# Summing the last experts' results in a graph and mixture-of-experts kernel: GpSimd's additions go to VectorE and TensorE, and three one-hot matrices are made earlier

## The chip, the cores and the metric

The kernel runs on one core of a Trainium2 chip. The metric is the device time of one execution in microseconds; a change is judged by the median of several executions.

## What is computed

The reference takes 384 nodes of 512 features and 6144 edges and applies eight layers, each added to its input. Seven of them (four graph layers, three feed-forward ones) lie before the change. The last one is a mixture of 64 experts, of which each node uses 8:

```python
w, idx = _gate(x2, gate_w, gate_b)          # 8 of 64 experts and their weights, for each node
h = silu(einsum('ecd,edm->ecm', xb, w1)) * einsum('ecd,edm->ecm', xb, w3)
yb = einsum('ecm,emd->ecd', h, w2)
y = yb.at[flat_e, pos].get(...) * w.reshape(-1)[:, None]
return y.reshape(T, K, DIM).sum(1)          # each node: the sum of its 8 weighted results
```

The change is in that last sum over a node's results and the addition to `x`. All data is fp32 at this point.

## The kernel before

The 384 nodes are three tiles of 128 rows (`NT = 3`); `x[:, t, :]` is the running result, 128 x 512 for each tile `t`. The experts are sorted by how many nodes chose them. Expert 0 of that order is computed densely; the other 63 form 38 blocks of at most 128 rows, each of one expert (128 rows) or of two (64 rows each). The loop over `BLOCKS` near line 1616 takes one block per turn. Block 34 is of one expert, 35 and 36 are of two, and 37, the last, is of one.

In turn i the loop does, in this order: start the loads of later experts (SP's DMA queue), gather the rows of block i+4 (GpSimd, indirect DMA), `hidden(i)` on TensorE (tile `mm`), the SiLU on ScalarE and the product `hide` on VectorE, `turned(i+1)` (TensorE, tile `tp`, copied to `xe` by ScalarE), then `output(i-1)`: TensorE multiplies by the second weight and VectorE scales the rows by the routing weight into `ye`. Then `turned_hidden(i)` turns `hide` on TensorE and VectorE copies it to `hT`.

Up to block 34, `output` ends with a scatter by GpSimd: each row of `ye` goes to its own place in `parts`, a DRAM tensor of 384 x 8 rows. For the last three blocks (`DIRECT = 3`) there is no scatter. Instead `placed` makes a one-hot matrix on VectorE (tile `turn`, 128 x 384: which node each row belongs to), and TensorE multiplies it with `ye` into `sums[t]`, one accumulator in PSUM for each tile.

At the end of turn 35 `gathered_back(t)` brings `parts` back: for each tile two DMAs of 1 MB on SP's queue, each with four of the node's eight rows, into the weight buffers that have come free (so the profile names them `w<-parts`). For tiles 0 and 1 GpSimd then adds the second half to the first (128 x 2048 elements). After the loop VectorE adds the four remaining rows of each tile to `x` (`summed`), while for tile 2 the second half is added on TensorE, by multiplying with the identity into `sums[2]`. Last, VectorE adds `sums[t]` to `x[:, t, :]`, and ScalarE's queue stores it to `out`.

What sets the order: from line 1197 on every engine's instructions are issued in the order in which the program writes them (the class `InTurn`, whose helper is line 88; so most lines of the profile show L88, and operations must be told apart by their tiles). SP's queue likewise takes its DMAs in the order written. An engine that waits holds all that is written behind it on that engine.

Profile names: `mm`, `acc` accumulators; `ye` scaled results; `hT` the turned hidden; `turn` the one-hot; `x<-x,w` the additions of returned rows on VectorE; `acc<-w,ident` those on TensorE; `acc<-ye,turn` the matmuls of `placed`; `w<-w,w` the additions on GpSimd; `x<-x,acc` the last sums.

Of the kernel before, what the change touches and what calls it, by code (L numbers as in the profile page):

```python
# [8 lines left out]
F32 = mybir.dt.float32  # L9
# [4 lines left out]
OP = mybir.AluOpType  # L14
AX = mybir.AxisListType

P = 128
N = 384
# [24 lines left out]
DIRECT = 3  # L43
# [6 lines left out]
BLOCKS, _ones, _left = _ones[:3], _ones[3:], _twos[:]  # L50
# [43 lines left out]
def gnn_ffn_kernel(ctx: ExitStack, tc: tile.TileContext, a, out: bass.AP):  # L94
    nc = tc.nc
    V, S, G, T = nc.vector, nc.scalar, nc.gpsimd, nc.tensor
# [5 lines left out]
    def slot(i=None):  # L102

        if i is None:
            i, turns_of_slots[0] = turns_of_slots[0] % W_BUFS, turns_of_slots[0] + 1
        return wpool.tile([P, 4 * D], F32, name=f"w8_{i}")
# [20 lines left out]
    x = const.tile([P, NT, D], F32, name="x")  # L127
# [79 lines left out]
    def row(name, n=D, pool=None):  # L207

        v = a[name]
        r = (pool or rows).tile([P, n], F32, name="row" if pool is None else "row_" + name)  # L210
        nc.scalar.dma_start(r, bass.AP(tensor=v.tensor, offset=v.offset, ap=[[0, P], [1, n]]))
        return r
# [4 lines left out]
    ident = const.tile([P, P], F32, name="ident")  # L217
# [5 lines left out]
    nodes = const.tile([P, N], F32, name="nodes")  # L223
# [96 lines left out]
    with ExitStack() as s1:  # L320
# [102 lines left out]
        with tc.tile_pool(name="pa", bufs=1, space=bass.MemoryType.PSUM) as pa:  # L423
# [19 lines left out]
            sums, counts = {}, []  # L443
# [39 lines left out]
            for c in range(EC):  # L483
# [34 lines left out]
                for h in range(by_scalar(c)):  # L518
                    j = ep.tile([P, 2 * HD0], F32, name="junk", bufs=2)
                    summed = S.activation(j, g3[:, h, :], AF.Identity, accum_out=w8[:, h:h + 1])  # L520
                marks.append(summed)

                with tc.issue_after(done.ins):
# [16 lines left out]

            plain = T, V, S, G
            T, V, S, G = (InTurn(tc, *e) for e in zip(plain, (counts[-1], done, summed, scattered)))
            wv = stream.take(ahead=False)

# [49 lines left out]
    with ExitStack() as s2:  # L594
# [321 lines left out]
        T, V, S, G = plain  # L916
# [26 lines left out]
    for i in range(3):  # L943
# [3 lines left out]
        if i > 0:  # L947
            w = stream.take()
            pw = [ps.tile([P, D], F32, name="mm") for t in range(NT)]
            for k in range(KC):  # L950
                for t in range(NT):
                    T.matmul(pw[t], lhsT=hT[:, k, t * P:(t + 1) * P], rhs=w[:, k, :], start=k == 0,  # L952
                             stop=k == KC - 1)
# [7 lines left out]
        back = [ps.tile([P, D], F32, name="mm") for t in range(NT)] if i == 2 else None  # L961
        for f in range(KC):
# [8 lines left out]
            j = qp.tile([P, N], F32, name="sq")  # L971
# [67 lines left out]
    with tc.issue_after(shown.ins):  # L1039
        b = row("L2_gnn_b")  # L1040
# [25 lines left out]
    moe = ctx.enter_context(tc.tile_pool(name="moe", bufs=2))  # L1066
# [101 lines left out]
    b = row("L3_gnn_bias")  # L1168
# [28 lines left out]
    T, V, S, G = (InTurn(tc, engine) for engine in plain)  # L1197
# [142 lines left out]
    for b in BLOCKS:  # L1340
        for r in b:
            if r >= STATIC:
                free.sort()
                end, i = free.pop(0)
# [3 lines left out]
    def load(i):  # L1348

        for r, n, end in firsts.pop(i, []):  # L1350
            load_expert(r, n)
            seconds.append((r, n, end))
        while seconds and seconds[0][2] + 2 <= i and (len(seconds) > 2 or not firsts):
            r, n, end = seconds.pop(0)
            load_second(r, n)
# [36 lines left out]
    tables, chosen, sources, numbers = {}, {}, {}, {}  # L1392
# [30 lines left out]
    def numbered(g, p):  # L1423

        blocks = GROUPS[g]
        n = len(blocks)
        num = ex.tile([P, n], F32, name=f"num{g}", bufs=1)
        none = ex.tile([P, n], F32, name=f"none{g}", bufs=1)
        src = ex.tile([P, n], I32, name=f"src{g}", bufs=1)
        node = ex.tile([P, n], F32, name=f"node{g}", bufs=1)  # L1430
        for h, c in enumerate(parts_of(blocks)):
            V.tensor_reduce(num[c], p[c, :, h, 0:2], AX.X, OP.add)
        V.tensor_scalar(none, num, 0.0, FAR, op0=OP.is_equal, op1=OP.mult)
        V.scalar_tensor_tensor(node, num, -1.0, none, op0=OP.add, op1=OP.add)
        V.tensor_copy(src, node)
        numbers[g] = num, none, node
        for i, b in enumerate(blocks):
            sources[b] = src[:, i:i + 1]
# [19 lines left out]
    def gather(i):  # L1458
        G.indirect_dma_start(out=rows_of[i % AHEAD], out_offset=None, in_=xnd,
                             in_offset=bass.IndirectOffsetOnAxis(ap=sources[BLOCKS[i]], axis=0),  # L1460
                             bounds_check=N - 1, oob_is_err=False)

    def turned(i):
        p = pt.tile([P, KC, P], F32, name="tp")
        r = rows_of[i % AHEAD].rearrange("c (p k) -> c k p", k=KC)
        for k in range(KC):
            T.transpose(p[:, k, :], r[:, k, :], ident)
        xe = ex.tile([P, KC, P], F32, name="xe")
        S.copy(xe, p)
        return xe  # L1470
# [4 lines left out]
    def hidden(b, xe):  # L1475
        p = ps.tile([P, 2, 2 * P], F32, name="mm")
        for k in range(KC):
            for c, r in zip(halves(b), b):
                T.matmul(p[c], lhsT=xe[:, k, c], rhs=experts_w[r][0][:, :, k, :], start=k == 0, stop=k == KC - 1)
        hid = ex.tile([P, 2 * P], F32, name="hide")  # L1480
        S.activation(hid, p[:, 0, :], AF.Silu)
        V.tensor_mul(hid, hid, p[:, 1, :])
        return hid
# [25 lines left out]
    def placed(i, ye):  # L1509

        b = BLOCKS[i]
        if not sums:
            sums.extend(ps2.tile([P, D], F32, name="acc") for t in range(NT))
        to = moe.tile([P, N], F32, name="turn", bufs=2)
        V.tensor_scalar(to, nodes, tables[b][2], None, op0=OP.is_equal)
        for t in range(NT):
            T.matmul(sums[t], lhsT=to[:, t * P:(t + 1) * P], rhs=ye, start=b == BLOCKS[-DIRECT],
                     stop=t < 2 and b == BLOCKS[-1])

    view = parts.rearrange("(t p j) d -> t p j d", t=NT, p=P)  # L1520
    back = []

    def gathered_back(t):

        halves_ = []
        for h in range(2):
            i = rooms.pop(0)
            r = (slot(i) if i < W_BUFS else more[0].tile([P, 4 * D], F32, name=f"w8_{i}")).rearrange(
                "p (j d) -> p j d", j=4)
            nc.sync.dma_start(r, view[t, :, 4 * h:4 * h + 4, :])  # L1530
            halves_.append(r)
        if t < 2:
            first, second = halves_
            G.tensor_tensor(first, first, second, op=OP.add)
        back.append(halves_)

    def summed(t):
        for j in range(4):
            V.tensor_add(x[:, t, :], x[:, t, :], back[t][0][:, j, :])


    place = moe.tile([P, NT, E3], F32, name="place", bufs=1)
# [7 lines left out]
    def ranked(turn, dst):  # L1550
        p = ps.tile([P, NT, E3], F32, name="mm")
        for t in range(NT):
            T.matmul(p[:, t, :], lhsT=turn[:, t * P:(t + 1) * P], rhs=perm, start=True, stop=True)
        S.copy(dst, p)
# [56 lines left out]
    sums = []  # L1611
# [4 lines left out]
    for i, b in enumerate(BLOCKS):  # L1616


        load(i)
        if 2 <= i and i + AHEAD < len(BLOCKS):  # L1620
            gather(i + AHEAD)
        hid = hidden(b, xes.pop(i))
        if i + 1 < len(BLOCKS):
            xes[i + 1] = turned(i + 1)
        if i == 0:
            numbered(4, told_slots(4, slice(0, 2)))
            gather(3)
            gather(4)
            ranked(turns[1], weight)
        if i in told_at:  # L1630
            to_use = told_at[i], told_slots(told_at[i])
            chosen.pop(told_at[i])

        if i == 1:
            table(*to_use)
            to_use = None
        if i == EXCEED:
            exceeded()
        sent = output(*waiting) if waiting is not None else None
        waiting = i, turned_hidden(hid)  # L1640
        if sent is not None:
            placed(*sent)
        if to_use is not None:
            table(*to_use)
            to_use = None
        if i == 0:
            tell(place0, pick, slice(0, STATIC))
        if i == 1:
            choose(1)
            tell(place, weight, slice(STATIC, E3))  # L1650
        if i == 2:
            gather(5)

        for j in range(i + 1, min(i + AHEAD + 3, len(BLOCKS))):
            g = group_of[BLOCKS[j]]
            if i >= 3 and g not in known and i + 1 not in told_at:
                known.add(g)
                choose(g)
                told_at[i + 1] = g
        if i + 1 == EXCEED:  # L1660
            V.tensor_scalar(hasb, place, 0.5, None, op0=OP.is_gt)
        if i == len(BLOCKS) - DIRECT:
            free.sort()
            rooms = [n for _, n in free]
            for t in range(NT):
                gathered_back(t)
    summed(0)
    placed(*output(*waiting))
    for j in range(4):
        T.matmul(sums[2], lhsT=ident, rhs=back[2][1][:, j, :], start=False, stop=j == 3)  # L1670
    summed(1)
    summed(2)
    for t in range(NT):
        V.tensor_add(x[:, t, :], x[:, t, :], sums[t])
        nc.scalar.dma_start(out[t * P:(t + 1) * P, :], x[:, t, :])
    T, V, S, G = plain
# [71 lines left out]
```

## Time and profile before

| | us |
|---|---|
| median of 3 runs (lowest to highest) | 853.11 (850.22 to 855.66) |
| profiled execution, its own time | 855.45 |
| span of that execution in the trace | 853.5 |
| TensorE, VectorE, ScalarE, GpSimd busy | 746.5, 462.1, 273.1, 234.5 |
| six returning transfers `w<-parts`, median from issue to landing | 11.6 |
| GpSimd's two additions of 128 x 2048 | 4.50 and 4.88 |
| last sum of VectorE ends | 847.97 |

The span is the time between the first and the last recorded event; the execution's own time has 1.95 us around it. Times in the trace count from the span's start. Each record has an engine, an operation, the tiles it writes and reads, its duration, and the idle time of its engine before it with the event that ended it. A matmul of fp32 data is recorded as two passes, so "x6" of `acc<-ye,turn` is three matmuls. Records that the timeline merges in one row carry the time from the first's start to the last's end. "issue" in the chain of waits is time for which the profile shows no cause. The granted clock of TensorE is 1.00 at full speed.

### The profile page before, as it was taken

The numbers are of one execution on the slowest core, as the hardware profiler recorded it, in microseconds if no ns is written. First come the engines' busy times: TensorE is split into PE (matmuls) and PEld (weight loads), VectorE is DVE, ScalarE is ACT, GpSimd is POOL, SyncE is SP. The second block draws the span as 40 slices with busy tenths as digits, with TensorE's granted clock in tenths as the row PEclk, the third lists the DMA queues.
The fourth block names the chain that finished last, engine by engine and source line by source line (L and its number), as shares of the span: only waits on it lengthen the run. The fifth ranks groups of instructions, "written<-read, shape, count | busy, mean of one in ns | idle before, by whom it ended". The sixth has DMA issues, their size and how long they took to land.

```text
span 853.5 us, 9894 instructions
## 1 busy us (share of the span) xinstructions
PE 746.5 (87%) x2865; PEld 350.2 (41%) x2865; DVE 462.1 (54%) x1199; ACT 273.1 (32%) x1042; POOL 234.5 (27%) x230
## 2 busy tenths in 40 slices
PE   5999888898946769948789999799999999999975
PEld 3444433343434535423355544454444344333432
DVE  4575988887779665376522254745434242421227
ACT  1144766666638723333131111221111111011100
POOL 0046777777600210000100000023333233322122
PEclk9999999899968678985989999889999999999998
DMA  9987877877388011210531463298999999999982
GB/s 336 410 312 243 284 273 258 285 216 238 106 330 311 1 37 53 96 50 12 226 138 49 154 215 108 90 390 320 408 408 403 400 387 396 385 389 391 379 338 104
DMA packets 71197, 211.84 MB, mean 248 GB/s; under 512 B 11615, under 2 KB 16351, under 8 KB 70368
## 3 DMA queue, kind: packets, MB, share of 16 engines
q1 hardware_dynamic: 40592, 135.56, 41.7%
q0 software_dynamic: 19728, 57.97, 19.8%
q10 hardware_dynamic: 10816, 17.61, 5.9%
q8 instruction: 25, 0.41, 0.2%
q14 instruction: 36, 0.29, 0.1%
HBM read 188.46 MB, written 29.83 MB: 256 GB/s over the span
## 4 chain that ended last, share of the span: by engine, by line
PE 56%; DVE 20%; DMA 14%; ACT 6%; issue 3%; DVEq 0%; POOL 0%; SPq 0%; ACTq 0%; POOLq 0%
PE mm L88 14%; DMA w<-in_L_ffn_w_dram 11%; PE acc L88 9%; PE mm L290 8%; PE mm L461 6%; PE mm L1080 4%; PE acc L1093 3%; PE tp L88 3%; PE mm L463 2%; PE mm L952 2%; DVE gp L507 2%; PE acc L965 2%; ACT junk L520 2%; DVE gp L509 2%; DVE mx L88 2%
## 5 line engine op out<-in xcount | busy, mean ns | idle before, releaser
L88 PE MATMUL mm<-w,xe 128*64 128x512 f32 (+1 forms) x504 | 146.1, 598 | 4.9 <-DMA w<-in_L_ffn_w_dram 4.9
L461 PE MATMUL mm<-w,osT 128*128 128x512 bf16 x378 | 92.2, 391 | 9.9 <-ACT osT L386 9.8
L88 POOL DMA_INDIRECT xg<-xnd,src x38 | 39.3, 1034 | 164.9 <-DVE ye L88 140.8
L88 ACT ACTIVATE hide<-mm 128x256 f32<-128x256 f32 x38 | 14.6, 385 | 214.1 <-PE mm L88 214.1
L88 POOL DMA_INDIRECT parts<-ye,dst x35 | 37.9, 1083 | 154.9 <-DVE ye L88 154.9
L88 PEld LDWEIGHTS mm<-w,xe 128*64 128x64 f32 (+1 forms) x504 | 48.2, 148 | 75.0 <-issue 69.1
L88 PE MATMUL acc<-w,hT 128*64 128x512 f32 (+1 forms) x244 | 77.4, 610 | 0.0
L88 DVE TENSOR_TENSOR hide<-hide,mm 128x256 f32<-128x256 f32 x38 | 16.1, 424 | 109.0 <-ACT hide L88 109.0
L290 PE MATMUL mm<-w,xT 128*128 128x512 f32 x144 | 68.6, 633 | 1.8 <-DMA w<-in_L_gnn_Ww_dram 1.2
L520 ACT ACTIVATE junk<-gp 128x128 f32<-128x128 f32 x186 | 54.8, 296 | 39.8 <-issue 22.9
L436 POOL DMA_INDIRECT gq<-qd,dsti x48 | 50.6, 1054 | 59.8 <-DMA qd<-gq 41.8
L461 PEld LDWEIGHTS <-osT 128*128 128x128 bf16 x378 | 36.7, 100 | 65.8 <-issue 17.1
L446 POOL DMA_INDIRECT mat<-w,kidx x48 | 57.0, 1187 | 22.5 <-DMA mat<-w,kidx 4.4
L88 DVE TENSOR_SCALAR ye<-acc,wts 128x512 f32<-128x512 f32 x35 | 26.3, 750 | 59.4 <-PE acc L88 59.4
L520 ACT ACTIVATE junk<-relu 128x128 f32<-128x128 f32 x147 | 43.4, 297 | 18.3 <-DVE relu L516 10.6
L290 PEld LDWEIGHTS mm<-w,xT 128*128 128x128 f32 x144 | 28.8, 204 | 37.7 <-issue 34.4
L516 DVE SCALAR_TENSOR_TENSOR relu<-mm,wa_relu 128x512 f32<-128x512 f32 x42 | 28.1, 684 | 29.3 <-PE mm L463 29.3
L463 PE MATMUL mm<-gq,ident 128*128 128x512 f32 x84 | 43.2, 596 | 0.0
L88 PEld LDWEIGHTS tp<-ident,xg 128*128 128x128 f32 x164 | 23.6, 202 | 28.5 <-issue 24.5
L465 PE MATMUL pc<-od,os 128*128 128x384 bf16 x144 | 29.3, 330 | 6.3 <-DVE od L372 6.3
L520 ACT ACTIVATION_READ_ACCUMULATOR junk<-gp 128x1 f32 x186 | 34.8, 187 | 0.0
L509 DVE SCALAR_TENSOR_TENSOR gp<-gp,wa_relu 128x1024 f32<-128x1024 f32 x27 | 33.1, 1228 | 0.9
(370 smaller groups left out, 1210.0 us busy)
## 6 DMA issues: line engine op xcount, KB each, us to landing
w<-in_L_ffn_w_dram SPq DMA_DIRECT2D x204, 512.0 KB, 12.0
mat<-y ACTq DMA_DIRECT2D x2, 4608.0 KB, 28.4
m<-mat SPq DMA_DIRECT2D x12, 768.0 KB, 7.1
parts<-xg POOLq DMA_DIRECT2D x1, 6144.0 KB, 19.9
w<-parts SPq DMA_DIRECT2D x6, 1024.0 KB, 11.6
w<-in_L_gnn_Ww_dram SPq DMA_DIRECT2D x4, 1024.0 KB, 10.1
w<-in_L_gnn_W_dram ACTq DMA_DIRECT2D x2, 1024.0 KB, 9.0
qd<-gq SPq DMA_DIRECT2D x3, 516.0 KB, 6.7
```

The costliest lines, as they stand in the source:

```text
L88: self.last = getattr(self.engine, name)(*args, **kwargs)
L290: last = T.matmul(p, lhsT=xT[:, k, t * P:(t + 1) * P], rhs=w(k), start=start and k == 0, stop=stop and k == kc - 1)
L436: G.indirect_dma_start(out=gq, out_offset=None, in_=qd, in_offset=bass.IndirectOffsetOnAxis(ap=dsti[:, c:c + 1], axis=0))
L446: return G.indirect_dma_start(out=mats[c % 2], out_offset=bass.IndirectOffsetOnAxis(ap=kidx[:, c:c + 1], axis=0), in_=sums.pop(c), in_offs ...
L461: T.matmul(z[h], lhsT=osT[:, t, :], rhs=split[t][:, i, cs], start=t == 0 and i == 0, stop=False)
L463: T.matmul(z[h], lhsT=ident, rhs=gq[:, cs], start=False, stop=True)
L465: counts.append(T.matmul(pc[t], lhsT=os_[:, t * P:(t + 1) * P], rhs=od, start=c == 0, stop=c == EC - 1))
L509: done = V.scalar_tensor_tensor(g3, g3, 0.0, wide, op0=OP.max, op1=OP.mult)
L516: done = V.scalar_tensor_tensor(g3[:, c8, :], z[h].rearrange("p (h k) -> p h k", h=HH), 0.0, wide[:, c8, :], op0=OP.max, op1=OP.mult)
L520: summed = S.activation(j, g3[:, h, :], AF.Identity, accum_out=w8[:, h:h + 1])
L1080: T.matmul(p, lhsT=gate[:, k, c], rhs=xT[:, k, :], start=k == 0, stop=k == KC - 1)
L1093: T.matmul(p, lhsT=hid[:, m, t * P:(t + 1) * P], rhs=w2[:, m, :], start=m == 0, stop=m == 1)
```

## The change

GpSimd's additions are removed. For tiles 0 and 1 VectorE adds all eight returned rows; for tile 2 TensorE adds five by the identity and VectorE three. Five of the additions of tile 0 are issued at the end of turn 36, ahead of block 37's `hide` on VectorE; the others follow the loop, around the last `output`. The one-hot matrices of blocks 35, 36 and 37 are made at the end of turn 34 by a new function `destined`, with one more buffer (`to`).

```diff
@@ placed
-        to = moe.tile([P, N], F32, name="turn", bufs=2)
-        V.tensor_scalar(to, nodes, tables[b][2], None, op0=OP.is_equal)
+        to = tos[b]
@@ gathered_back
-        if t < 2:
-            first, second = halves_
-            G.tensor_tensor(first, first, second, op=OP.add)
         back.append(halves_)
-    def summed(t):
-        for j in range(4):
-            V.tensor_add(x[:, t, :], x[:, t, :], back[t][0][:, j, :])
+    def added_back(t, js):
+        for j in js:
+            V.tensor_add(x[:, t, :], x[:, t, :], back[t][j // 4][:, j % 4, :])
+    def added_too(t, js):
+        for j in js:
+            T.matmul(sums[t], lhsT=ident, rhs=back[t][j // 4][:, j % 4, :], start=False, stop=j == js[-1])
+    tos = {}
+    def destined(b):
+        tos[b] = moe.tile([P, N], F32, name="to", bufs=1) if len(tos) == 2 else             moe.tile([P, N], F32, name="turn", bufs=2)
+        V.tensor_scalar(tos[b], nodes, tables[b][2], None, op0=OP.is_equal)
@@ the loop over the blocks, at the end of a turn
+        if i == len(BLOCKS) - DIRECT - 1:
+            for b in BLOCKS[-DIRECT:]:
+                destined(b)
         if i == len(BLOCKS) - DIRECT:
             free.sort()
             rooms = [n for _, n in free]
             for t in range(NT):
                 gathered_back(t)
-    summed(0)
+        if i == len(BLOCKS) - 2:
+            added_back(0, range(5))
+    added_back(0, range(5, 8))
+    added_back(1, range(3))
     placed(*output(*waiting))
-    for j in range(4):
-        T.matmul(sums[2], lhsT=ident, rhs=back[2][1][:, j, :], start=False, stop=j == 3)
-    summed(1)
-    summed(2)
-    for t in range(NT):
+    added_too(2, range(3, 8))
+    added_back(1, range(3, 8))
+    for t in range(NT):
+        if t == 2:
+            added_back(2, range(3))
         V.tensor_add(x[:, t, :], x[:, t, :], sums[t])
         nc.scalar.dma_start(out[t * P:(t + 1) * P, :], x[:, t, :])
```

## The prediction

> **What bounds the kernel now.** I read the page's chain first, then the chain of waits of the last 35 us, then the timeline of each engine there, then each transfer's landing, then the windows with the granted clock. The diff touches nothing before about 805 us, and the instruction order of every engine and queue up to there is the same in both kernels, so the first 805 us stay as they are. Up to 813.5 us the chain is the stream of expert weights: TensorE waits last on `w<-in_L_ffn_w_dram`. From there nothing more is loaded from the weights, and the end is set by three engines handing blocks 35, 36 and 37 to one another. The chain there, in columns start, duration, what:
>
> ```profile
> 829.38 0.03 DVE ye L88
> 829.42 0.64 issue
> 830.05 0.41 DVE hT L88
> 830.47 2.21 DVE turn L88
> 832.67 0.61 DVE x L88
> 833.29 0.02 issue
> 833.31 4.89 DVE x L88
> 838.20 0.02 issue
> 838.22 0.70 DVE x L88
> 838.92 0.02 issue
> 838.95 0.04 DVE x L88
> 838.98 0.57 issue
> 839.56 0.74 DVE ye L88
> ```
>
> Two pieces stand out: a one-hot (`turn`) of 2.2 us and one addition of 4.9 us, where their neighbours take 0.41 and 0.70. The timeline of GpSimd and VectorE says why:
>
> ```profile
> 827.96 4.50 POOL L88 TENSOR_TENSOR w<-w,w 128x2048 f32<-128x2048 f32 x1 [14.55 <-DMA w<-parts]
> ...
> 830.38 2.29 DVE L88 TENSOR_SCALAR turn<-nodes,node 128x384 f32<-128x384 f32 x1
> 832.60 7.04 DVE L88 TENSOR_TENSOR x<-x,w 128x512 f32<-128x512 f32 x4
> 832.73 4.54 PE L88 MATMUL acc<-ye,turn 128*128 128x512 f32 x6 [2.96 <-DVE turn L88]
> 832.76 4.88 POOL L88 TENSOR_TENSOR w<-w,w 128x2048 f32<-128x2048 f32 x1 [0.30 <-DMA w<-parts]
> ```
>
> The one-hot ends when GpSimd's first addition ends (832.46), and the 4.9 us addition when its second does (837.64). VectorE stands still under GpSimd, and TensorE behind VectorE: its 2.96 us wait is on `turn`. The windows' row shows that this also cost clock (columns: window, length, busy time of PE, PEld, DVE, ACT, POOL, granted clock, DMA share, GB/s):
>
> ```profile
> 829.80:832.70 2.90, 0.00 (x0) 0.00 (x0) 2.90 (x4) 0.00 (x0) 2.65 (x1) 1.00 1.01 421
> 832.70:837.10 4.40, 4.37 (x6) 1.83 (x7) 4.37 (x2) 0.00 (x0) 4.34 (x1) 0.61 0.65 266
> 838.98:840.68 1.70, 0.01 (x1) 0.00 (x1) 1.70 (x4) 0.00 (x0) 0.00 (x0) 1.00 0.00 0
> ```
>
> After 2.9 us without a matmul, six passes took 4.4 us at a clock of 0.61; after 1.7 us the next six took 2.68 (840.68 to 843.36) at 1.00.
>
> **When the data comes back.** The six 1 MB transfers of `parts` are issued at 818.6, 819.0, 819.5, 820.0, 820.7 and 821.5 and need 5.5, 8.6, 10.6, 12.6, 14.4 and 16.1 us to land: 824.1, 827.6, 830.1, 832.6, 835.1, 837.6. The second, asked for alone:
>
> ```profile
> L1530 SPq DMA_DIRECT2D w<-parts x1: 424/424/424, 819.0 to 819.0; - x1
> ...
> DMA to landing us min/median/max: 8.6/8.6/8.6
> ```
>
> GpSimd, which waited for it, began at 827.96, so a landing is seen 0.1 to 0.4 us after that figure. SP waits for the last scatter to land before it issues the first (its longest wait there is 7.2 us on `parts<-ye,dst`); neither is moved, so these six times hold for the new kernel.
>
> **The change, step by step.**
>
> *The three one-hots go in front, to VectorE after 805.2 us.* They cost 3 x 0.33 (step of one to the next, 820.73 to what follows, is 0.33 to 0.41) = 1.0 to 1.2 us where VectorE is idle for 4.17 us, until `hide` at 809.41. Cost nothing; without that cover it would be 1.2 us. [...]
>
> *What stands free on TensorE.* `placed` of block 35 no longer waits for its one-hot (done 821.15), only for `ye` (820.48): 0.65 us earlier. `hidden` of block 37 then ends at 826.75, not 827.40, and its `hide` could run on VectorE at 827.28.
>
> *The new wait.* VectorE now has five additions of tile 0 in front of that `hide`: four on the first transfer (seen 824.1 to 824.5, done by 827.3), the fifth on the second (827.96, as GpSimd saw it), done at 828.66. Behind it stand `hide`, `ye` of block 36, `hT` of block 37, and TensorE's transposes of `hide`. `hide` ends at 829.06, so the transposes start at 829.16; before they started at 829.27. The 0.65 us are thus given back almost wholly, and the cover is gone: any later landing of that transfer moves everything after it.
>
> *Block 36.* `ye` 829.08, `hT` 829.75 (0.67 after it, as in 829.38 to 830.05), done at 830.08. No one-hot follows, so `placed(36)` starts on TensorE at 829.88 instead of 832.73: 2.85 us gained. With a gap of 0.2 us and not 2.9, it runs at full clock: 3 x 0.86 = 2.57 us, to 832.45; block 37's output follows, and `ye` starts 1.95 us later (1.92 to 1.99 in earlier blocks), at 834.4.
>
> *VectorE meanwhile.* Three additions of tile 0 and three of tile 1 (third transfer, 830.1): 830.08 + 6 x 0.70 = 834.3. It is ready just as the output is, so `ye(37)` starts at 834.4 instead of 839.56: 5.15 us gained, of which 1.9 + 4.2 = 6.1 are the two stalls, less additions that GpSimd no longer makes.
>
> *The end.* `placed(37)` runs on TensorE from 835.2 to 837.77, its one-hot being there. Then five, not four, additions by the identity (10 passes of 0.43, the last 0.59) take to 842.2; the one on the fifth transfer comes first (835.1), those on the sixth from 838.6 (landed 837.6, 0.6 us of slack at the least). VectorE: 835.1 + 5 x 0.70 = 838.6, two sums by 839.8, three additions by 841.9, and the last sum waits for TensorE until 842.56 (0.33 after its end, as before: 846.96 to 847.29). Before it started at 847.29: 4.7 us gained. TensorE's fifth addition costs 0.86 of that.
>
> *The store.* The three output transfers were issued at 846.82, 847.41 and 848.4; the second issue took 0.84 us and held the third 0.4 us, and the third landed in 3.3 us where the first took 2.5. Now the first two leave near 839.3 and 839.9, so the third is alone: 0.4 + 0.7 = 1.1 us more at most.
>
> Sum: 4.7 + 1.1 = 5.8 us. The profiled execution took 855.45 us (span 853.5); it would be 849.65. The median of the runs is 853.11, 2.3 below it; since the end of the kernel repeats in each, I take the same 5.8 off: **847.3 us**, 0.7% faster. VectorE has 19 additions for 12 and still ends earlier.
>
> **Rivals.**
>
> [...]
>
> *VectorE becomes the bound.* Additions beside transfers at 420 GB/s might cost more than the 0.70 of rows taken when DMA stood still. From the fifth on, twelve stand on VectorE's chain before the transfers and their neighbours end (1 + 6 + 5); with 0.65 us of slack (841.9 to 842.56) each 0.1 us more costs up to 1.2. At 0.35 more each the gain is 5.8 - 12 x 0.35 + 0.65 = 2.25: 850.9 us. Against it: `hide` took 0.42 under 420 GB/s, as elsewhere.
>
> *Slower: the second transfer is late.* One mechanism, at the fifth addition: `hide`, `ye`, `hT` and TensorE's transposes are queued behind it, so each us by which it is seen after 827.96 adds one. From 833.8 (15.2 us to landing and not 8.6) the gain is used up. That takes transfers that share the engines in turn and land together near 836: 855.3 us, with 2.2 us lost. Against it: the landings are about 2.5 us apart, one after the other.
>
> *The change doesn't do what it says* would be 853 us: stalls with another cause than GpSimd. The two ends that coincide speak against it.
>
> **How the numbers follow.** The forecast 0.74, the clock 0.10, VectorE as the bound 0.08, no effect 0.04, the late transfer 0.04. Runs of the kernel before lie from 850.2 to 855.7, so a median of a few may be off by 2 us, and landings are seen 0.4 us early or late: the forecast alone reaches from 844.2 to 850.0. To hold 8 in 10 over the cases the range is **844.0 to 851.5 us**, which takes in the clock's case and most of VectorE's. A measurement can tell about 1% from no change, 8.5 us here: faster than 844.6 needs more gain than the path has, or luck in the runs (0.11); slower than 861.6 needs the late transfer at its worst (0.03); the rest, 0.86, is within 1%.
>
> **What would show it.** Right: no GpSimd instruction after 813; 19 `x<-x,w` additions of about 0.70, with DMA in the idle column before them; `hide` of block 37 released by VectorE's fifth addition near 828.7; `placed(36)` near 829.9 with a clock of 1.00; `ye(37)` near 834.4; last sum near 842.6; span near 847.7. Wrong: additions of 1 us or more beside transfers, a clock under 1 after 835, a second landing after 829, or a later first issue of the six transfers on SP.

## The result, and the profile after

| | before | after |
|---|---|---|
| median of 22 runs each, us | 852.1 | 845.47 |
| ratio after to before (95% interval) | | 0.9937 (0.9918 to 0.9956) |
| span of the profiled execution, us | 853.5 | 847.5 |
| first matmul after the last weights | 813.52 | 813.58 |
| last sum ends | 847.97 | 842.86 |
| from the end of the last sum to the end of the span | 5.53 | 4.64 |

The ratio is a gain of 5.4 us (3.7 to 7.0). The two traces run within 0.06 us of each other up to the last weights, so all of the 6.0 us by which the spans differ lies behind 813.5: 5.17 in the hand-over of the last blocks and 0.89 in the store. The chain of waits of the changed kernel (start, duration, what) is now TensorE almost without a break:

```profile
828.79 0.76 DVE ye L88
829.55 0.04 issue
829.59 2.84 PE acc L88 x6
832.43 1.73 PE mm L88 x4
834.16 0.03 issue
834.19 0.76 DVE ye L88
834.95 0.04 issue
834.99 7.15 PE acc L88 x16
842.14 0.02 issue
842.17 0.69 DVE x L88
```

VectorE's pieces of 2.2 and 4.9 us are gone, and what remains of it here is `ye`, twice, and the last sum. The timeline of VectorE shows the additions in their new places (start, duration, operation, idle before it and who ended that):

```profile
824.15 2.87 DVE L88 TENSOR_TENSOR x<-x,w 128x512 f32<-128x512 f32 x4 [3.28 <-DMA w<-parts]
827.30 0.69 DVE L88 TENSOR_TENSOR x<-x,w 128x512 f32<-128x512 f32 x1 [0.28 <-DMA w<-parts]
827.91 0.41 DVE L88 TENSOR_TENSOR hide<-hide,mm 128x256 f32<-128x256 f32 x1
828.79 0.75 DVE L88 TENSOR_SCALAR ye<-mm,wts 128x512 f32<-128x512 f32 x1 [0.46 <-PE mm L88]
829.45 0.41 DVE L88 COPY hT<-tp 128x256 f32<-128x256 f32 x1
829.78 4.19 DVE L88 TENSOR_TENSOR x<-x,w 128x512 f32<-128x512 f32 x6
834.19 0.75 DVE L88 TENSOR_SCALAR ye<-mm,wts 128x512 f32<-128x512 f32 x1 [0.22 <-PE mm L88]
```

Block 37's `hide` follows the fifth addition at once and ends at 828.32. TensorE's transposes of it start at 828.67, right behind the matmuls before them and without a wait:

```profile
828.67 0.50 PE L88 MATMUL tp<-ident,hide 128*128 128x128 f32 x2
```

So the wait that the change added is covered, by about a third of a microsecond. VectorE's six additions end 0.22 us before the output for `ye(37)` is there. The returned rows' additions on VectorE from 804 us on (busy time and mean in ns), and windows of TensorE (granted clock third from the end, then the DMA's share and its GB/s):

```profile
L88 DVE TENSOR_TENSOR x<-x,w 128x512 f32<-128x512 f32 x19 | 13.0, 690 | 4.0 <-DMA w<-parts 3.6
```

```profile
829.59:832.43 2.84, 2.84 (x7) 1.41 (x8) 2.77 (x5) 0.00 (x0) 0.00 (x0) 1.00 0.99 404
834.15:834.99 0.84, 0.00 (x0) 0.00 (x0) 0.80 (x2) 0.00 (x0) 0.00 (x0) 1.00 0.98 410
834.99:842.14 7.15, 7.13 (x16) 2.96 (x16) 6.50 (x10) 0.00 (x0) 0.00 (x0) 1.00 0.29 111
```

Nineteen additions take a mean of 690 ns, and the six that run beside transfers of some 404 GB/s take 4.19 us together, 0.70 each. The longest gap of TensorE behind the last weights is 0.84 us, and the clock is 1.00 to its last matmul.

### The profile page after: what moved, and what is told of

It is laid out like the page before. It is cut to its first block, busy times and chain, and to the rows that moved or that the text cites. A ratio compares the mean times of both kernels' runs of the same rounds, so it can differ in the third digit from the quotient of the medians.

```text
span 847.5 us, 9900 instructions
## 1 busy us (share of the span) xinstructions
PE 743.4 (88%) x2867; PEld 348.0 (41%) x2867; DVE 462.4 (55%) x1206; ACT 273.0 (32%) x1042; POOL 231.7 (27%) x228
## 4 chain that ended last, share of the span: by engine, by line
PE 55%; DMA 18%; DVE 18%; ACT 6%; issue 2%; POOL 0%; SPq 0%; DVEq 0%; ACTq 0%; POOLq 0%
DMA w<-in_L_ffn_w_dram 14%; PE mm L88 12%; PE acc L88 9%; PE mm L290 8%; PE mm L461 6%; PE mm L1080 4%; PE acc L1093 3%; PE mm L463 3%; PE tp L88 3%; PE mm L952 2%; DVE gp L507 2%; PE acc L965 2%; ACT junk L520 2%; DVE gp L509 2%; DVE mx L88 2%
## 5 line engine op out<-in xcount | busy, mean ns | idle before, releaser
L436 POOL DMA_INDIRECT gq<-qd,dsti x48 | 52.9, 1103 | 59.9 <-DMA qd<-gq 42.0
L430 POOL DMA_INDIRECT gp<-pd,srci x27 | 30.6, 1132 | 15.1 <-DMA pd<-gp 6.8
## 6 DMA issues: line engine op xcount, KB each, us to landing
mat<-y ACTq DMA_DIRECT2D x2, 4608.0 KB, 28.6
```

The costliest lines, as they stand in the source:

```text
L430: G.indirect_dma_start(out=gp, out_offset=None, in_=pd, in_offset=bass.IndirectOffsetOnAxis(ap=srci[:, c:c + 1], axis=0))
L436: G.indirect_dma_start(out=gq, out_offset=None, in_=qd, in_offset=bass.IndirectOffsetOnAxis(ap=dsti[:, c:c + 1], axis=0))
```

## The experiments

The runs went to other chips, whose times up to the last weights are 11 to 17 us longer (3 us in the trace of "balanced"). So ratios are to the kernel before on the same chip, and places in the trace are counted from TensorE's first matmul after the last weights, where all kernels agree: the scaling of block 35 starts 6.2 us behind it in each. Each row has one trace. Behind that point the landings of the returning transfers move a little from trace to trace: GpSimd's first addition, which waits for the second, starts 14.4 us behind it in the kernel before and 13.5 to 14.2 in the four other traces that have it. Differences of half a microsecond between kernels with GpSimd can be that alone. All in us:

| kernel | placed(36) starts | ye(37) starts | wait of TensorE before placed(37) | placed(37) takes | last sum starts | ratio to before (95%) |
|---|---|---|---|---|---|---|
| before | 19.2 | 26.0 | 1.69 | 2.84 | 33.8 | 1 |
| after | 16.0 | 20.6 | 0.84 | 2.84 | 28.6 | 0.9937 (0.9918 to 0.9956) |
| one-hots only | 16.0 | 25.6 | 5.79 | 5.23 | 35.1 | 0.9998 (0.9981 to 1.0016) |
| VectorE only | 17.3 | 22.9 | 2.11 | 2.84 | 33.5 | 0.9993 (0.9974 to 1.0013) |
| additions late | 16.0 | 23.9 | 4.16 | 5.49 | 34.9 | 0.9984 (0.9960 to 1.0008) |
| one-hots back | 17.3 | 21.9 | 1.17 | 2.84 | 30.2 | 0.9954 (0.9934 to 0.9973) |
| GpSimd beside | 16.0 | 27.2 | 7.42 | 4.43 | 36.8 | 1.0064 (1.0032 to 1.0096) |
| gap filled | 18.7 | 25.1 | 3.10 | 4.54 | 34.2 | 1.0010 (0.9985 to 1.0034) |
| late, filled | 16.0 | 23.9 | 0.73 | 2.84 | 31.9 | 0.9977 (0.9957 to 0.9997) |
| before, filled | 18.8 | 25.6 | 0.82 | 2.84 | 33.3 | 1.0005 (0.9979 to 1.0031) |
| after, again | 16.0 | 20.6 | 0.84 | 2.84 | 28.6 | 0.9945 (0.9927 to 0.9962) |
| balanced | 16.0 | 20.6 | 0 | 2.84 | 27.9 | 0.9948 (0.9923 to 0.9974) |
| scaled on ScalarE | 16.0 | 20.5 | 0 | 2.84 | 27.0 | 0.9920 (0.9893 to 0.9946) |

**One-hots only.** The three one-hots in front, GpSimd still adding.

```diff
 # the kernel before
-        V.tensor_scalar(to, nodes, tables[b][2], None, op0=OP.is_equal)   # in placed
+        to = tos[b]
+        if i == len(BLOCKS) - DIRECT - 1:
+            for b in BLOCKS[-DIRECT:]:
+                destined(b)
```

> The kernel before with one part of the change: the three one-hots are made at the end of turn 34, GpSimd still adds. Theory (GpSimd's hold on VectorE is what sets the end; the one-hots matter only once it is gone): the one-hot of block 36 no longer stalls, so placed(36) starts about 2.9 us earlier, near 829.6, but the first addition now waits to 832.5 and the second to 838.2, so ye(37) stays at 839.6; only the one-hot of block 37 (0.33 to 0.4 us) leaves the path: span 853.1, gain 0.4. Rival (the path is placed(36) and what it feeds): gain 2.8, span 850.7.

No gain. placed(36) starts 3.2 us earlier, as in the changed kernel, and nothing comes of it. VectorE and TensorE from the timeline, TensorE in a fence of its own:

```profile
849.58 7.05 DVE L88 TENSOR_TENSOR x<-x,w 128x512 f32<-128x512 f32 x4 [2.30 <-POOL w L88]
856.55 0.74 DVE L88 TENSOR_SCALAR ye<-mm,wts 128x512 f32<-128x512 f32 x1
```

```profile
857.35 5.23 PE L88 MATMUL acc<-ye,to 128*128 128x512 f32 x6 [5.79 <-DVE ye L88]
```

The stall has only changed its victim: the first addition waits 2.30 us for GpSimd's first result, and the four take 7.05 us beside its second addition, as they did before (7.04), so `ye(37)` stands at 25.6. TensorE, done sooner, waits 5.8 us instead, and then needs 5.2 us for six passes, at a clock of 0.54. Those slow passes were not expected; with them the last sum is 1.3 us later than before.

**VectorE only.** GpSimd's additions gone, VectorE adding eight rows in the old places.

```diff
 # the kernel before
-            G.tensor_tensor(first, first, second, op=OP.add)
-        for j in range(4):
-            V.tensor_add(x[:, t, :], x[:, t, :], back[t][0][:, j, :])
+        for j in range(8 if t < 2 else 4):
+            V.tensor_add(x[:, t, :], x[:, t, :], back[t][j // 4][:, j % 4, :])
```

> The kernel before with the other part alone: GpSimd's two additions are gone and VectorE adds all eight rows of tiles 0 and 1, in the old places after the loop; one-hots and tile 2 as before. Theory (the gain is in where VectorE's additions stand, not in the stall alone): placed(36) near 830.8, eight additions of 0.70 from 830.7 to 836.4 hold ye(37) there (before 839.6), then twelve more of 0.70 and three sums end near 847.7, against 847.97: VectorE becomes the bound, span 853.2, gain 0.3. Rival (the stall of 6.1 us is the gain): span near 848.5, gain 5.

The theory holds: the stall is gone and the time is the same. VectorE's timeline:

```profile
843.41 0.41 DVE L88 TENSOR_SCALAR turn<-nodes,node 128x384 f32<-128x384 f32 x1
843.74 5.76 DVE L88 TENSOR_TENSOR x<-x,w 128x512 f32<-128x512 f32 x8
849.42 0.74 DVE L88 TENSOR_SCALAR ye<-mm,wts 128x512 f32<-128x512 f32 x1
850.08 0.41 DVE L88 TENSOR_SCALAR turn<-nodes,node 128x384 f32<-128x384 f32 x1
850.41 8.54 DVE L88 TENSOR_TENSOR x<-x,w 128x512 f32<-128x512 f32 x12
```

The one-hot is back at 0.41 and each addition at 0.70. But twenty of them stand behind `hT(37)`, VectorE works there without a pause, and the last sum starts at 33.5, hardly before the 33.8 of the kernel before. So neither removing the stall nor preparing the one-hots is the gain by itself.

**Additions late.** The changed kernel without the five early additions.

```diff
 # the changed kernel
-        if i == len(BLOCKS) - 2:
-            added_back(0, range(5))
-    added_back(0, range(5, 8))
+    added_back(0, range(8))
```

> The changed kernel with one thing undone: the five additions of tile 0 that stand ahead of block 37's hide go behind the loop, so eleven stand there ahead of ye(37). Theory (the early additions are needed, since ye(37) is behind them): 829.8 + 11 x 0.70 = 837.5 for ye(37), not 834.2; TensorE's placed(37) and five identity additions follow 3.3 us later, span 850.8. Rival (TensorE alone is the bound and VectorE has room): 847.5.

`ye(37)` came 3.3 us later, to the tenth as worked out, but the last sum 6.3 us later. The windows show the rest, before placed(37), during it and behind it:

```profile
850.37:854.53 4.16, 0.00 (x0) 0.00 (x0) 4.06 (x7) 0.00 (x0) 0.00 (x0) 0.89 0.33 138
854.53:860.02 5.49, 5.49 (x7) 2.39 (x8) 5.32 (x9) 0.00 (x0) 0.00 (x0) 0.50 0.11 40
860.02:864.61 4.59, 4.59 (x10) 1.65 (x9) 1.17 (x2) 0.00 (x0) 0.00 (x0) 0.95 0.21 73
```

If the clock is either 1.00 or 0.50, a mean of 0.89 over 4.16 us is 0.9 us at half: by this estimate it fell about 3.2 us into the wait. It was at half for the whole of placed(37) (0.50 over 5.49) and (0.95 over 4.59) for some 0.5 us more, an estimated 6.9 us in all.

**One-hots back.** The changed kernel with `turn` made in `placed` again (the diff of "one-hots only", reversed, on the changed kernel).

> The changed kernel with the one-hots back in placed. Theory: the one-hot of block 35 costs nothing (VectorE waits for the second transfer anyway before hide(37)); those of blocks 36 and 37 each put 0.33 to 0.4 us plus the wait on the path of VectorE and TensorE: placed(36) near 830.8 (829.6), placed(37) near 836.5 (835.0), span 849.0, loss 1.5. Rival (they were covered by VectorE's waits for data and cost nothing): 847.5.

As the theory had it: placed(36) at 17.3 and placed(37) at 23.1, the last sum 1.65 us later (1.5 expected). So the one-hots in front are worth 1.6 us, in the company of the other parts.

**GpSimd beside.** The changed kernel with GpSimd adding the same halves into two free buffers.

```diff
 # the changed kernel, after gathered_back
+            for t in range(2):
+                n = rooms.pop(0)
+                spare = ...            # a free weight buffer, read by nobody
+                G.tensor_tensor(spare, back[t][0], back[t][1], op=OP.add)
```

> The changed kernel, with GpSimd's two additions of 128 x 2048 put back beside it: they add the same returned halves of tiles 0 and 1 into buffers that nobody reads, so no result waits for them. Theory (GpSimd's addition holds VectorE's instructions with two inputs in SBUF): GpSimd runs from about 828 to 832.5 and from about 833 to 837.6; the six additions after hT(37), from 829.8, are held to 832.5, then one passes, then held to 838; ye(37) near 841 (834.2), span near 854, loss 6 to 7. Rival (VectorE only waited for GpSimd's result): no change, 847.5.

This settles what GpSimd does to VectorE: nobody waits for its result, and yet the additions do. VectorE, then GpSimd:

```profile
842.00 0.75 DVE L88 TENSOR_SCALAR ye<-mm,wts 128x512 f32<-128x512 f32 x1 [0.28 <-PE mm L88]
842.66 0.41 DVE L88 COPY hT<-tp 128x256 f32<-128x256 f32 x1
843.00 11.07 DVE L88 TENSOR_TENSOR x<-x,w 128x512 f32<-128x512 f32 x6
853.98 0.74 DVE L88 TENSOR_SCALAR ye<-mm,wts 128x512 f32<-128x512 f32 x1
```

```profile
840.94 9.79 POOL L88 TENSOR_TENSOR w<-w,w 128x2048 f32<-128x2048 f32 x2 [14.27 <-DMA w<-parts]
```

Six additions take 11.07 us and not 4.19, 6.9 more, where 6 to 7 were expected; `ye` and `hT`, which read PSUM, ran at 0.75 and 0.41 in the midst of it. The slower clock in placed(37) (0.63) then took 1.6 more (4.43 for 2.84).

**Gap filled.** The kernel before with three matmuls ahead of placed(36), whose output is not read.

```diff
 # the kernel before, after turned_hidden of block 37
+            idle = pt.tile([P, D], F32, name="tp")
+            for j in range(3):
+                T.matmul(idle, lhsT=ident, rhs=rows_of[3], start=True, stop=True)
```

> The kernel before, with three matmuls of 128x512 by the identity after the transposes of block 37's hide; their output is not read. They fill TensorE's gap of 2.9 us. Theory: the granted clock stays at 1.00 from 832.7 to 837 (before 0.61), placed(36) takes 2.7 us and not 4.5, but ye(37) waits for VectorE's additions until 839.6 all the same: span 853.5, no change. [...] If the clock falls without a gap, the gap was not its cause.

No change in time, but not quite for the reason given. The clock stayed at 1.00 through placed(36); TensorE then came to its next wait earlier, that wait grew from 1.69 to 3.10 us, and the clock fell behind it: placed(37) took 4.54 us at 0.62. A gap filled in one place opened in the next. `ye(37)` is 0.9 us earlier than in the kernel before only because GpSimd began that much earlier in this trace (13.5 and not 14.4); the last sum is 0.5 us later all the same.

**Late, filled, and before, filled.** The same filling ahead of placed(37): four matmuls in the kernel with the late additions, three (with three ahead of placed(36)) in the kernel before.

```diff
 # additions late
-    placed(*output(*waiting))
+    last = output(*waiting)
+    idle = pt.tile([P, D], F32, name="tp")
+    for j in range(4):
+        T.matmul(idle, lhsT=ident, rhs=rows_of[3], start=True, stop=True)
+    placed(*last)
```

> The run with the late additions, with four matmuls by the identity, whose output is not read, between block 37's output and placed(37): they fill the gap of 4.2 us in which TensorE waits for VectorE there. Theory (a wait of TensorE costs twice: its length, and the halved clock behind it): ye(37) stays at 23.9 us after the last weights, placed(37) takes 2.8 and not 5.5 us, the last sum starts near 32.0 and not 34.9. Rival (those matmuls are slow for another reason, such as the transfers or the accumulators): 34.9 or later.

> The kernel before with both of TensorE's late gaps filled by three matmuls each whose output is not read, ahead of placed(36) and of placed(37). Theory: the clock stays at 1.00 to the end, but ye(37) still waits for VectorE behind GpSimd; TensorE ends near 32.6 us after the last weights and VectorE's own additions and sums end at 33.6, against 34.5: of the change's 5.2 us in this stretch at most 1 is the clock's. Rival (the clock's fall is a main part of what the change saves): last sum ends near 32, gain 2 or more.

The first confirms that the wait causes the fall: with `ye(37)` in the same place, placed(37) takes 2.84 us at a clock of 1.00, and the last sum starts at 31.9 and not 34.9.

```profile
854.20:857.04 2.84, 2.84 (x7) 1.40 (x8) 2.70 (x5) 0.00 (x0) 0.00 (x0) 1.00 0.03 6
```

The second shows how much of the change's gain was the clock's: next to nothing. With both late gaps of TensorE filled the kernel before has its last sum at 33.3, 0.4 us earlier, and GpSimd began 0.4 us earlier in this trace too (14.0 and not 14.4): VectorE is behind GpSimd all the same.

**After again, balanced, and scaled on ScalarE.** Two kernels that are carried on from the changed one; the changed kernel ran once more on the same chip as the second of them, while "balanced" ran on another.

```diff
 # balanced
+        if i == len(BLOCKS) - 1:
+            S.activation(ye, p, AF.Copy, scale=tables[b][1])   # else VectorE as before
-    placed(*output(*waiting))
-    added_too(2, range(3, 8))
-    added_back(1, range(3, 8))
+    last = output(*waiting)
+    T.matmul(sums[1], lhsT=ident, rhs=back[1][1][:, 3, :], start=False, stop=False)
+    placed(*last)
+    added_too(2, range(4, 8))
+    added_back(1, range(3, 7))
-            added_back(2, range(3))
+            added_back(2, range(4))
 # scaled on ScalarE, on top of it
-        if i == len(BLOCKS) - 1:
+        if i >= len(BLOCKS) - 2:
+        if i == len(BLOCKS) - 1:
+            added_back(0, range(5, 6))                          # ahead of hT(37)
-    added_back(0, range(5, 8))
+    added_back(0, range(6, 8))
-    added_too(2, range(4, 8))
+    added_too(2, range(5, 8))
+    added_back(2, range(1))                                     # ahead of the first two sums
-            added_back(2, range(4))
+            added_back(2, range(1, 5))
```

> The changed kernel itself, on the same chip as the two carried on from it: 0.9937 of the kernel before, last sum started 28.6 us after the last weights.

> The changed kernel carried on: ye(37) is scaled by ScalarE, which is idle, one identity addition (tile 1's last row, back at 832.6) goes into TensorE's gap ahead of placed(37), and tile 2 has four rows on TensorE and four on VectorE. Theory (TensorE's chain sets the end, with a gap of 0.84 us before placed(37) and five identity additions of 0.43 x 2 behind it): last sum near 841.2 (842.17), span 846.5, gain 1.0. Rival (ScalarE's scaling or VectorE's extra addition takes it back): 847.5 or a little more.

> The balanced kernel carried on: ye(36) is scaled by ScalarE as well, VectorE puts one addition of tile 0 in its place, and tile 2 has three rows on TensorE and five on VectorE. Theory (both engines are full to the end, so each 0.7 us taken off one and each matmul moved counts): last sum starts near 27.3 us after the last weights (27.9, and 28.6 in the changed kernel), 0.15% below the changed kernel. Rival (VectorE becomes the bound, or its addition holds hT(37)): 27.9 or later.

The last sum starts at 28.6, 27.9 and 27.0: 0.7 us where 1.0 was expected, and 1.6 where 1.3 was. ScalarE scales in 0.69 us, where VectorE needs 0.75:

```profile
839.56 0.69 ACT L88 ACTIVATE ye<-mm,wts 128x512 f32<-128x512 f32 x1 [1.49 <-PE mm L88]
844.89 0.69 ACT L88 ACTIVATE ye<-mm,wts 128x512 f32<-128x512 f32 x1 [4.65 <-PE mm L88]
```

In the last one both engines are then full from 16 us to the end. Its time is below that of the kernel before by more than the interval. Against the changed kernel on the same chip the ratios order the same way, 0.9920 and 0.9945, but their intervals overlap: the 1.6 us are read from the traces, and the times don't show them.

## Why the prediction was right, and where it was off

**The sum.** Forecast were 5.8 us, to a span of 847.7; the span came out at 847.5, and the ratio gives 5.4 (3.7 to 7.0). That the spans fit so closely is in part luck: the last sum gains 5.2 us where 4.7 were forecast, the store 0.9 where 1.1 were, and the trace of the kernel before is the one in which GpSimd begins latest (14.4 us; at the 14.0 of "before, filled" the last sum came 0.4 us sooner). The median of the kernel before moved from 853.11 to 852.1 with more runs, 1.0 of the 1.8 us by which 845.47 lies below the 847.3 forecast; the rest is within the interval.

**The six landings.** Right in order and to 0.1 us for four of them (5.4, 12.6, 14.4 and 16.2 us), with SP's first issue at 818.69 against 818.62. The second and the third landed half a microsecond sooner than in the kernel before: 8.1 and 10.1 us for 8.6 and 10.6.

**One-hots in front cost nothing.** Right. They ran at 805.2 to 806.4, the last one in 0.55 us and not 0.41, beside a scatter issued by GpSimd, which took 1.01 us as before and landed in 6.2 us (before 6.3). Where the 0.14 us come from, no run shows.

**The new wait.** Right in place, too high in price. The prediction took the second transfer as seen when GpSimd began, 827.96; VectorE began at 827.30. So 0.6 of the 0.65 us gained on block 35 were kept (the transposes of `hide` at 828.67, not 829.16). The mis-sized term is 0.5 us in the safe direction, and most of it is luck, since the landing itself came half a microsecond sooner in this execution; the rest fits with GpSimd beginning later than VectorE on the same transfer (by 0.24 us in the run "GpSimd beside", where both wait for it). How thin the cover is shows in the balanced kernel, where the transfer was seen 14.2 us behind the last weights and not 13.7: there TensorE did wait 0.15 us for `hide`.

**Blocks 36 and 37.** `placed(36)` 829.59 (829.88), `ye(37)` 834.19 (834.4), last sum 842.17 (842.56): 0.2 to 0.4 us early. For the first two it is that term. For the last sum most of it is a misreading: the prediction let it start 0.33 us behind TensorE's end "as before", but in the kernel before it was VectorE's own two sums ahead of it that held it, with no wait for TensorE, which was done at 846.96:

```profile
843.36 3.60 PE L88 MATMUL acc<-w,ident 128*128 128x512 f32 x8
846.10 1.88 DVE L88 TENSOR_TENSOR x<-x,acc 128x512 f32<-128x512 f32 x3
```

In the changed kernel it does wait for TensorE, and starts 0.03 us behind it (842.14). The additions cost 0.70 each beside transfers of 404 GB/s, so the rival in which VectorE becomes the bound falls in this kernel; it is what happens in the one with VectorE only, because of where the additions stand and not because each costs more. In the rival of the late transfer there is a slip: the gain would be used up by a landing after 14.4 us (8.6 and 5.8), not 15.2; nothing else hangs on it.

**The store.** 1.1 us at most were taken; 0.89 in this pair. From the end of the last sum to the end of the span it took 4.6 to 4.9 us in most kernels whose last store leaves well behind the others and 5.05 to 5.5 in the three that store all tiles together (before, VectorE only, before filled), but 5.45 in the second trace of the changed kernel. So it is worth about half a microsecond and isn't sure in one execution.

**The clock.** The forecast went by the rows of the kernel before, where the clock fell behind a wait of 2.96 us (0.61) and not behind one of 1.69 (1.00). That was right: behind 3.10 us it fell again (0.62, "gap filled"), behind 2.11 it did not (1.00, "VectorE only"). The clock's case in the chances and the range, 1.8 us of slow passes (4.4 less 2.6 in the kernel before) in the changed kernel too, was the author's estimate, and the changed kernel doesn't show it: its clock is 1.00 from the last weights to its last matmul. The price of 1.8 us, moreover, holds only for a short stretch at half clock, such as the 3.4 us estimated from 0.61 over 4.40 us in the kernel before. With the late additions the stretch was an estimated 6.9 us, of which 6.0 fell on matmuls, and the price 3.0 us (34.9 to 31.9). And the slow passes of the kernel before, which are gone in the changed one (placed(36) takes 2.84 us and not 4.54), were no part of the gain: they weren't on its path, as the filled gaps show.

**What the sum didn't say.** It added stalls of 6.1 us "less additions that GpSimd no longer makes". The runs show that no part stands alone. One-hots alone and the stall's removal alone give 0 within 0.3%. With the stall gone, one-hots in front and one more row of tile 2 on TensorE, but no early additions, it is 0.9984 (0.9960 to 1.0008). Only with the five additions in the 6.8 us in which VectorE had waited for block 37's `hide` is it 0.994. The one row of tile 2 that moved to TensorE was not taken back alone, so its part isn't known.

## What to carry to other kernels

When an engine that helps another holds it as well (beside GpSimd six of VectorE's additions took 11.07 us and not 4.19), count what the helper saves against where the helped engine would put the work: here seven more additions on VectorE were free, because five of them fit into a wait for block 37 and the rest into TensorE's time. Price a wait of TensorE near the end twice, its length and the slow passes behind it (4.16 us and then 3.0 with the late additions), and see whether a wait that is filled opens again at the next hand-over (1.69 us became 3.10 in "gap filled"). Ask, too, which engine the last sum waits for: slow passes of another engine cost nothing here (with TensorE's late gaps filled the kernel before has a ratio of 1.0005). A part that gives nothing alone isn't refuted: run it with its partners, and read both in the trace from a common point, since 1 to 2 us of 850 don't show in the times.

## What the runs showed of the hardware

GpSimd's addition of 128x2048 from SBUF (4.5 to 5.1 us) held VectorE's additions of two SBUF operands (six in 11.07 for 4.19 us) and, in the kernel before, its one-hot from SBUF to SBUF (2.29 for 0.41 us), with no data between them; `hide`, `ye` and `hT`, which read PSUM, ran at 0.41, 0.75 and 0.41 beside it in the run "GpSimd beside". In the 0.30 us between the two GpSimd additions of the kernel before one of VectorE's got through (0.61 us in the chain, the next 4.89).

Waits of TensorE up to 2.11 us in this stretch left the clock at 1.00; from 2.96 us on it fell (2.96, 3.10, 4.16, 5.79 and 7.42). Rows of the runs "gap filled" (placed(37)) and "GpSimd beside" (the wait, then placed(37)):

```profile
851.17:855.71 4.54, 4.54 (x7) 2.00 (x8) 4.37 (x7) 0.00 (x0) 0.00 (x0) 0.62 0.01 4
847.36:854.78 7.42, 0.00 (x1) 0.01 (x1) 7.32 (x7) 0.00 (x0) 3.37 (x1) 0.76 0.20 81
854.78:859.21 4.43, 4.43 (x7) 2.05 (x8) 4.29 (x7) 0.00 (x0) 0.00 (x0) 0.63 0.02 4
```

If the clock is either 1.00 or 0.50, as in the rows that lie wholly on one side (1.00 in "late, filled", 0.50 in "additions late"), these means give an estimate of the time at half: some 3.4 us behind the waits of 2.96 and 3.10, and 6.8 to 6.9 us for the three longer ones (the wait of 5.79 has 0.83, and the 5.23 us behind it 0.54). In the longer ones it began by this estimate 3.2 to 3.9 us into the wait, so the longest wait, 7.42 us, had half of it behind it when the matmuls came, and cost them less (1.6 us) than that of 4.16 (3.0). Where between 2.1 and 3.0 us the line lies, and how it depends on where the wait falls, stays open.
